# Row maxima across four context quarters: PE transposes replaced by GpSimd copies between partitions, and absorbed query products tied to alternate row halves

## The chip, the cores and the metric

The program runs on one core of a Trainium2 chip. The metric is the device time of one execution in microseconds (us). A core has TensorE (PE, matrix products; PEld is its weight load), VectorE (DVE), ScalarE (ACT), GpSimd (POOL) and SyncE (SP, which issues most DMAs). SBUF and PSUM have 128 partitions. Each engine works through its own instructions in order and waits on semaphores for the others.

## What is computed

Four cross-attention blocks are applied one after the other to `x` (16 batches, 56 tokens, 256 wide) with one context (16 batches, 1500 keys, 128 wide). L0 is a single-head attention with a gate and a norm. L1 and L3 are 16-head attentions with a mask over the keys and a feed-forward part. L2 is a causal self-attention, a 16-head cross-attention over all 1500 keys, and two expert MLPs. In L1 and L3 the core is

```python
sim = jnp.einsum('bhid,bhjd->bhij', q, k)
sim = jnp.where(media_mask[:, None, None, :], sim, neg_inf)
attn = jax.nn.softmax(sim, axis=-1)
out = jnp.einsum('bhij,bhjd->bhid', attn, v)
```

and the softmax of L2's cross-attention is the same without a mask. The mask lets through only padded keys, which all lie among the last 384; the kernel tests for that at run time and takes its short branch, in which L1 and L3 look at 384 keys alone.

## The kernel before, in words

The 16 batches go through each layer in 4 groups of 4 (`G = 4`, 224 tokens a group). The keys of a batch are cut into four quarters (`NQ = 4`). A block of 32 query rows (tokens times heads, `BW = 32`) is multiplied with the four quarters by four products that write the four bands of 32 partitions of one PSUM tile `sc`: partition 32g + r holds query row r against quarter g (L338 to L343). So the maximum of a query row over all keys is a maximum over four partitions that lie 32 apart.

The unit of work is a *period* (`period`, L408): up to 14 such blocks in L1 and L3 (96 keys a quarter, five blocks to one `sc` tile), 8 or 4 in L2 (375 keys a quarter). Three periods are in flight. In period u the kernel

- makes the scores of u on PE (`scores_block`, L340) and copies them to the SBUF tile `p` on DVE, with the mask added and the maximum of each partition taken into `few` (L351 and L355 in L1 and L3; the one instruction of L345 in L2),
- turns the period before, x: exponentials on ACT with the shift as bias and the sum as a second output (`weights_of`, L382), then 32x32 transposes on DVE (`turn_blocks`, L393),
- sums the period before that, y: weights times values on PE (L796 in L1 and L3, L1134 in L2), followed by a copy on ACT.

The shift (minus the maximum over the four quarters, the same in all four bands) is made by `shift_of` in two steps. Step 0: PE transposes the maxima (L362), DVE reduces over the four quarters (L364) and writes the result three more times (L369). Step 1: PE transposes back (L374), and ACT copies the result from PSUM to SBUF (its copies all carry the helper's line L246). In L1 and L3 (`apart`) both steps of u stand in the middle of period u; in L2 the steps of x stand in the first two quarters of the following period. The PSUM tile `t` of the transposes is one of two that `turn()` hands out to many users.

`absorbed` (L693) makes the queries of L1 and L3 for a pair of batches, 16 times in all. Each call makes two groups of eight products (L703); products of even heads read partitions 0 to 63 and write one `t` tile, those of odd heads read partitions 64 to 127 and write the other. ACT (L246) and DVE (L714) copy the tiles to `qa`.

A scheduler orders the instructions of each engine when the program is built, from dependencies and its own estimates; a manual dependency without a semaphore ("NoSync") only fixes an order on one engine. `turn_blocks` has one such tie: turns go after the last copy of scores, or after L369.

Of the kernel before, what the change touches and what calls it, by code (L numbers as in the profile page):

```python
# [62 lines left out]
def tile_kernel(ctx: ExitStack, tc: tile.TileContext, a, layers=4, groups=NG):  # L63
# [29 lines left out]
    def turn():  # L93
        return psum(ps_t, "t")
# [150 lines left out]
    def scalar_copy(out, in_, scale=1.0):  # L245
        nc.scalar.activation(out, in_, AF.Copy, scale=scale)  # L246
# [84 lines left out]
    def scores_block(u, i):  # L331

        sc = psum(ps_s, "sc")
        w, each = u["w"], u["each"]
        some = range(i, min(i + each, u["n"]))
        for j in some:
            at = (j - i) * w
            for g in range(NQ):  # L338
                q, k = u["qk"](j, g)
                nc.tensor.matmul(  # L340
                    sc[g * BW : (g + 1) * BW, at : at + w], q, k, start=True, stop=True,
                    skip_group_check=True,
                )  # L343
        if each == 1:
            return nc.vector.tensor_tensor_reduce(  # L345
                u["p"][:, i, :w], sc[:, :w], u["mask"], 1.0, LOWEST,
                ALU.add, ALU.max, u["mx"][:, i : i + 1],
            ).ins.name
        m = len(some)
        p = u["p"][:, i : i + m]  # L350
        nc.vector.tensor_tensor(  # L351
            p, sc[:, : m * w].rearrange("p (i k) -> p i k", i=m),
            u["mask"].unsqueeze(1).to_broadcast([128, m, w]), ALU.add,
        )
        return nc.vector.tensor_reduce(u["mx"][:, i : i + m], p, AX.X, ALU.max).ins.name  # L355

    def shift_of(u, i):

        n = u["n"]
        if i == 0:  # L360
            u["t"] = turn()
            nc.tensor.transpose(u["t"][:n, :128], u["mx"], ident)  # L362
            nm = small.tile([128, 128], F32, tag="nm", bufs=1, name="nm")[:n]
            nc.vector.tensor_reduce(  # L364
                nm[:, :BW], u["t"][:n, :128].rearrange("k (g r) -> k r g", g=NQ), AX.X,
                ALU.max, negate=True,
            )
            u["nm"] = nm
            return nc.vector.tensor_copy(  # L369
                nm[:, BW:].rearrange("k (g r) -> k g r", r=BW),  # L370
                nm[:, :BW].unsqueeze(1).to_broadcast([n, NQ - 1, BW]),
            ).ins.name
        else:
            nc.tensor.transpose(  # L374
                u["t"][:, 128 : 128 + n], u["nm"], ident[:n, :n]
            )
            u["shift"] = few(n)
            scalar_copy(u["shift"], u["t"][:, 128 : 128 + n])

    def weights_of(u):  # L380
        for i in range(u["n"]):
# [26 lines left out]
    def period(u):  # L408

        x, y = line["turn"], line["sum"]  # L410
        if u:
            n = u["n"]
            blocks = u["blocks"]
            u["p"] = p_tile("p")[:, : n * blocks * BW].rearrange("p (i k) -> p i k", i=n)
            u["mx"] = few(n)
            if u["w"] < blocks * BW:
                nc.gpsimd.memset(u["p"][:, :, u["w"] :], 0.0)
        if y:
# [12 lines left out]
        if u and u["apart"]:  # L431


            for i in range(0, n, u["each"]):
                copied = scores_block(u, i)
            if x and "shift" not in x:
                shift_of(x, 0)
                shift_of(x, 1)
                weights_of(x)
            at = y["blocks"] // 3 if y else 0  # L440
            sums(0, at)
            if x:
                turn_blocks(x, 0, x["n"] // 3, copied)
            copied = shift_of(u, 0)
            sums(at, 2 * at)
            if x:
                turn_blocks(x, x["n"] // 3, 2 * x["n"] // 3, copied)
            shift_of(u, 1)
            sums(2 * at, 3 * at)
            if x:  # L450
                turn_blocks(x, 2 * x["n"] // 3, x["n"], copied)
        else:

            for i in range(4):
                for j in range(2 * i, min(2 * i + 2, n)) if u else ():
                    scores_block(u, j)
                if y:
                    sums(i * y["blocks"] // 4, (i + 1) * y["blocks"] // 4)
                if x and i < 2 and "shift" not in x:
                    shift_of(x, i)  # L460
                    if i:
                        weights_of(x)
                if x and i > 1:
                    at = -(-x["n"] // 2)
                    turn_blocks(x, (i - 2) * at, (i - 1) * at)
# [227 lines left out]
    def absorbed(name, qT, pr):  # L693
# [3 lines left out]
        qa = big.tile([128, 2, N, H], F32, tag="qa", name="qa")  # L697
        for j0 in range(0, 8, 4):

            halves = [turn() for _ in range(2)]  # L700
            for j in range(4):
                for e in range(2):
                    nc.tensor.matmul(  # L703
                        halves[e][:, j * TP : (j + 1) * TP],
                        wkT[e * 64 : (e + 1) * 64, j0 + j, :],
                        qT[e * 64 : (e + 1) * 64, j0 + j, tok],
                        start=True, stop=True,
                    )
            for e in range(2):
                for b in range(2):  # L710
                    src = halves[e][:, : 4 * TP].rearrange("p (j b n) -> p b n j", b=2, n=N)[:, b]
# [665 lines left out]
```

## Time and profile before

| what | value |
|---|---|
| median of 3 runs | 1779.35 us (1778.93 to 1781.23) |
| the profiled execution: time / span | 1781.89 / 1780.0 us |
| mean granted PE clock | 0.986 |
| L0 until about | 178 us |
| L1 mainly | 178 to 500 us |
| L2 mainly | 500 to 1400 us |
| L3 mainly | 1400 to 1780 us |
| L382, exponentials on ACT (x1344) | 588.4 us busy |
| L340, scores on PE, all shapes | 605.2 us busy |
| L703, absorbed products on PE (x512) | 57.1 us busy |
| POOL, whole program | 100.7 us busy, 222 instructions |

An fp32 product leaves two records, so 512 records of L703 are 256 products. Busy times of PE overlap, and the ends of its records are modelled; the distance between the starts of successive records is the safer measure. Periods can be told by L362, L364 and L374, which stand once in each of the 128 periods (64 in L1 and L3, 64 in L2).

### The profile page before, as it was taken

The page shows a single profiled execution, that of the slowest core. Times are in us where ns is not written, and L with a number is a line of the kernel's source. Part 1 is how long each engine was busy: PE and PEld are TensorE (multiplying, and loading weights), DVE is VectorE, ACT ScalarE, POOL GpSimd, SP SyncE. Part 2 cuts the span into 40 slices and gives each one's busy share as a digit, 9 for nine tenths or more (in the row PEclk, how much of TensorE's full clock was granted, in tenths as well). Part 3 has the DMA queues.
Part 4 walks back from the last instruction along what each step waited for, and adds up shares of the span by engine and source line. Part 5 has one row for each costly group of instructions (what it writes and reads, how often), then busy time and mean ns, then how long its engine had stood idle before and what let it go on. Part 6 is the DMA issues. An engine that isn't in the chain of part 4 may idle for free.

```text
span 1780.0 us, 55805 instructions
## 1 busy us (share of the span) xinstructions
PE 1679.9 (94%) x24092; PEld 1109.0 (62%) x24092; DVE 1120.6 (63%) x2726; ACT 1018.4 (57%) x3577; POOL 100.7 (6%) x222
## 2 busy tenths in 40 slices
PE   4888999999899999999999999999999999999997
PEld 3566777776664556555665556556655767777765
DVE  2444866667755666767558675676577656666672
ACT  1443976757454356534755448456454876766763
POOL 0000000000011000000000000000000000000000
PEclk9999999999999999999999999999999999999998
DMA  7431213020030121000321012201200131212120
GB/s 182 132 101 45 76 30 105 23 88 24 28 132 21 37 96 46 21 20 20 99 68 36 5 34 90 78 29 49 91 21 11 34 137 48 92 47 94 44 68 8
DMA packets 60134, 107.08 MB, mean 60 GB/s; under 512 B 7430, under 2 KB 44822, under 8 KB 59878
## 3 DMA queue, kind: packets, MB, share of 16 engines
q1 hardware_dynamic: 58726, 97.27, 16.9%
q0 software_dynamic: 1152, 6.14, 1.4%
q8 instruction: 191, 3.13, 0.7%
q14 instruction: 65, 0.53, 0.1%
HBM read 102.49 MB, written 0.92 MB: 58 GB/s over the span
## 4 chain that ended last, share of the span: by engine, by line
PE 76%; DVE 12%; ACT 5%; DMA 3%; issue 2%; SPq 1%; POOL 1%; DVEq 0%; ACTq 0%; POOLq 0%
PE sc L340 21%; PE o L796 9%; DVE p L393 4%; PE mm L1167 4%; ACT p L382 4%; PE o L1134 4%; PE mm L859 3%; PE mm L847 3%; PE mm L832 3%; PE mm L683 3%; PE t L703 2%; PE mm L1180 2%; DVE p L345 2%; PE t L744 2%; PE t L752 2%; PE mm L883 2%
## 5 line engine op out<-in xcount | busy, mean ns | idle before, releaser
L382 ACT ACTIVATE p<-p,few 128x96 f32<-128x96 f32 (+1 forms) x1344 | 588.4, 440 | 7.1 <-ACT sums L246 0.3
L340 PE MATMUL sc<-kt,qa 128*32 128x375 f32 x3584 | 403.5, 484 | 12.5 <-DVE few L345 11.4
L393 DVE STREAM_TRANSPOSE p<-p 128x480 f32<-128x480 f32 (+3 forms) x319 | 317.2, 1004 | 58.9 <-ACT p L382 57.6
L345 DVE CUSTOM_DVE_ANT_0 p<-sc,no_mask 128x375 f32<-128x375 f32 x448 | 234.6, 534 | 85.0 <-PE sc L340 78.8
L382 ACT ACTIVATION_READ_ACCUMULATOR p<-p,few 128x1 f32 x1344 | 252.7, 188 | 0.0
L340 PE MATMUL sc<-ktl,qa 128*32 128x96 f32 x7168 | 201.7, 249 | 3.3 <-issue 1.7
L340 PEld LDWEIGHTS sc<-kt,qa 128*32 128x32 f32 x3584 | 117.9, 109 | 119.5 <-issue 67.2
L340 PEld LDWEIGHTS sc<-ktl,qa 128*32 128x32 f32 x7168 | 158.2, 110 | 35.5 <-issue 17.7
L1134 PEld LDWEIGHTS o<-p,vc 128*32 128x32 f32 x6144 | 134.7, 110 | 70.1 <-issue 49.8
L796 PE MATMUL o<-p,kvl 128*128 128x448 f32 x384 | 167.6, 565 | 1.1 <-DVE p L393 1.1
L1134 PE MATMUL o<-p,vc 128*32 128x64 f32 (+1 forms) x6144 | 153.0, 215 | 5.4 <-DVE p L393 4.0
L246 ACT ACTIVATE few<-t 128x14 f32<-128x14 f32 (+2 forms) x128 | 22.4, 175 | 233.3 <-PE t L374 233.2
L351 DVE TENSOR_TENSOR p<-sc,mkl 128x480 f32<-128x480 f32 (+1 forms) x192 | 113.8, 607 | 28.5 <-PE sc L340 28.2
L355 DVE TENSOR_REDUCE few<-p 128x5 f32<-128x480 f32 (+1 forms) x192 | 114.3, 612 | 2.8
L796 PEld LDWEIGHTS o<-p,kvl 128*128 128x128 f32 x384 | 67.1, 191 | 55.5 <-issue 45.1
L246 ACT ACTIVATE qa<-t 128x224 f32<-128x224 f32 (+1 forms) x96 | 38.7, 419 | 105.8 <-PE t L703 66.2
L1167 PE MATMUL mm<-xT,w 128*128 128x224 f32 (+1 forms) x384 | 80.9, 360 | 1.4 <-DMA w<-in_L_l_gate 1.0
L1167 PEld LDWEIGHTS mm<-xT,w 128*128 128x128 f32 (+1 forms) x384 | 65.6, 178 | 15.8 <-issue 6.0
L246 ACT ACTIVATE ot<-o 128x448 f32<-128x448 f32 x64 | 33.8, 528 | 54.0 <-PE o L796 54.0
L703 PE MATMUL t<-qT,wl 64*128 64x112 f32 x512 | 57.1, 287 | 2.7 <-DVE qa L714 2.0
L832 PE MATMUL mm<-w,oT 128*112 128x256 f32 x256 | 57.6, 380 | 0.4 <-DVE oT L758 0.4
L703 PEld LDWEIGHTS t<-qT,wl 64*128 64x128 f32 x512 | 49.2, 190 | 13.4 <-DVE qa L714 3.9
(262 smaller groups left out, 2287.6 us busy)
## 6 DMA issues: line engine op xcount, KB each, us to landing
w<-in_L_W SPq DMA_DIRECT2D x16, 1024.0 KB
kt<-in_ctxT SPq DMA_DIRECT2D x16, 768.0 KB
w<-in_L_Wq SPq DMA_DIRECT2D x8, 1024.0 KB
w<-in_L_Wo SPq DMA_DIRECT2D x8, 1024.0 KB
ktl<-in_ctxT SPq DMA_DIRECT2D x32, 192.0 KB
kvl<-in_ctx_last SPq DMA_DIRECT2D x32, 192.0 KB
w<-in_L_v_qkv SPq DMA_DIRECT2D x4, 768.0 KB
w<-in_L_l_qkv SPq DMA_DIRECT2D x4, 768.0 KB
```

The lines of the kernel that those rows point to most:

```text
L246: nc.scalar.activation(out, in_, AF.Copy, scale=scale)
L340: nc.tensor.matmul(sc[g * BW : (g + 1) * BW, at : at + w], q, k, start=True, stop=True, skip_group_check=True,)
L345: return nc.vector.tensor_tensor_reduce(u["p"][:, i, :w], sc[:, :w], u["mask"], 1.0, LOWEST, ALU.add, ALU.max, u["mx"][:, i : i + 1],).ins ...
L351: nc.vector.tensor_tensor(p, sc[:, : m * w].rearrange("p (i k) -> p i k", i=m), u["mask"].unsqueeze(1).to_broadcast([128, m, w]), ALU.add,)
L355: return nc.vector.tensor_reduce(u["mx"][:, i : i + m], p, AX.X, ALU.max).ins.name
L382: nc.scalar.activation(u["p"][:, i, : u["w"]], u["p"][:, i, : u["w"]], AF.Exp, bias=u["shift"][:, i : i + 1], accum_out=u["den"][:, i : i ...
L393: turned = nc.vector.transpose(blocks, blocks)
L703: nc.tensor.matmul(halves[e][:, j * TP : (j + 1) * TP], wkT[e * 64 : (e + 1) * 64, j0 + j, :], qT[e * 64 : (e + 1) * 64, j0 + j, tok], sta ...
L796: nc.tensor.matmul(o[:, : ub * BW], kv[:, j, :], p, start=start, stop=stop)
L832: nc.tensor.matmul(p[:TP, i * D : (i + 1) * D], oT[:, j, i * TP : (i + 1) * TP], wo[:, j, :], start=(j == 0), stop=(j == 7),)
L1134: nc.tensor.matmul(o[cols, : pieces * BW], made["v"][:, j, cols], p.rearrange("p (i g) r -> p g i r", g=4)[:, g], start=start, stop=stop, ...
L1167: nc.tensor.matmul(p[:w, k * T : (k + 1) * T], wt[:, c, cols], xe[n][:, c, :], start=(c == 0), stop=(c == 1),)
```

## The change

`shift_of` no longer uses PE. The tile `mx` gets four slots for each block; the partition maxima go to slot 0. GpSimd copies bands 1 to 3 of slot 0 to slots 1 to 3 of band 0, DVE takes minus the maximum over the slots in band 0, and GpSimd copies that result to the other three bands. The copies on GpSimd are each of 32 partitions by n elements (n = 14, 8 or 4). Both steps stand where step 0 stood. The tie of `turn_blocks` in L1 and L3 now always names the last copy of scores. In `absorbed` each product is tied behind the one before it, so that the two halves of the rows take turns.

```diff
-    def shift_of(u, i):
-        n = u["n"]
-        if i == 0:
-            u["t"] = turn()
-            nc.tensor.transpose(u["t"][:n, :128], u["mx"], ident)
-            nm = small.tile([128, 128], F32, tag="nm", bufs=1, name="nm")[:n]
-            nc.vector.tensor_reduce(
-                nm[:, :BW], u["t"][:n, :128].rearrange("k (g r) -> k r g", g=NQ), AX.X,
-                ALU.max, negate=True,
-            )
-            u["nm"] = nm
-            return nc.vector.tensor_copy(
-                nm[:, BW:].rearrange("k (g r) -> k g r", r=BW),
-                nm[:, :BW].unsqueeze(1).to_broadcast([n, NQ - 1, BW]),
-            ).ins.name
-        else:
-            nc.tensor.transpose(
-                u["t"][:, 128 : 128 + n], u["nm"], ident[:n, :n]
-            )
-            u["shift"] = few(n)
-            scalar_copy(u["shift"], u["t"][:, 128 : 128 + n])
+    def shift_of(u):
+        n, mx = u["n"], u["mx"]
+        shift = u["shift"] = few(n)
+        for g in range(1, NQ):
+            nc.gpsimd.tensor_copy(mx[:BW, g], mx[g * BW : (g + 1) * BW, 0])
+        nc.vector.tensor_reduce(
+            shift[:BW], mx[:BW].rearrange("p g i -> p i g"), AX.X, ALU.max, negate=True
+        )
+        for g in range(1, NQ):
+            nc.gpsimd.tensor_copy(shift[g * BW : (g + 1) * BW], shift[:BW])
...
-            u["mx"] = few(n)
+            u["mx"] = small.tile(
+                [128, NQ, n], F32, tag="mx", bufs=2, name="mx", padded_shape=[128, NQ, US]
+            )
...
-            copied = shift_of(u, 0)
+            shift_of(u)
             sums(at, 2 * at)
...
-            shift_of(u, 1)
             sums(2 * at, 3 * at)
...
-                if x and i < 2 and "shift" not in x:
-                    shift_of(x, i)
-                    if i:
-                        weights_of(x)
+                if x and "shift" not in x:
+                    shift_of(x)
+                    weights_of(x)
...
-            halves = [turn() for _ in range(2)]
+            halves, product_before = [turn() for _ in range(2)], None
             for j in range(4):
                 for e in range(2):
-                    nc.tensor.matmul(
+                    product = nc.tensor.matmul(
                         halves[e][:, j * TP : (j + 1) * TP],
...
+                    if product_before:
+                        tc.add_manual_dep(
+                            product.ins, product_before.ins.name,
+                            mybir.DependencyInfo(
+                                mybir.DependencyClass.NoSync, mybir.DependencyReason.DATA
+                            ),
+                            reason="halves of the rows go in turn",
+                        )
+                    product_before = product
```

More of the change, by code (lines that the diff above doesn't have):

```diff
@@ L346, in scores_block @@
                 u["p"][:, i, :w], sc[:, :w], u["mask"], 1.0, LOWEST,
-                ALU.add, ALU.max, u["mx"][:, i : i + 1],
+                ALU.add, ALU.max, u["mx"][:, 0, i : i + 1],
             ).ins.name
@@ L354, in scores_block @@
         )
-        return nc.vector.tensor_reduce(u["mx"][:, i : i + m], p, AX.X, ALU.max).ins.name
-    def shift_of(u, i):
-        n = u["n"]
-        if i == 0:
-            u["t"] = turn()
-            nc.tensor.transpose(u["t"][:n, :128], u["mx"], ident)
-            nm = small.tile([128, 128], F32, tag="nm", bufs=1, name="nm")[:n]
-            nc.vector.tensor_reduce(
-                nm[:, :BW], u["t"][:n, :128].rearrange("k (g r) -> k r g", g=NQ), AX.X,
-                ALU.max, negate=True,
-            )
-            u["nm"] = nm
-            return nc.vector.tensor_copy(
-                nm[:, BW:].rearrange("k (g r) -> k g r", r=BW),
-                nm[:, :BW].unsqueeze(1).to_broadcast([n, NQ - 1, BW]),
-            ).ins.name
-        else:
-            nc.tensor.transpose(
-                u["t"][:, 128 : 128 + n], u["nm"], ident[:n, :n]
-            )
-            u["shift"] = few(n)
-            scalar_copy(u["shift"], u["t"][:, 128 : 128 + n])
+        return nc.vector.tensor_reduce(u["mx"][:, 0, i : i + m], p, AX.X, ALU.max).ins.name
+    def shift_of(u):
[8 more added lines that the diff above has]
+            nc.gpsimd.tensor_copy(shift[g * BW : (g + 1) * BW], shift[:BW])
     def weights_of(u):
@@ L436, in period @@
             if x and "shift" not in x:
-                shift_of(x, 0)
-                shift_of(x, 1)
+                shift_of(x)
                 weights_of(x)
@@ L458, in period @@
                     sums(i * y["blocks"] // 4, (i + 1) * y["blocks"] // 4)
-                if x and i < 2 and "shift" not in x:
-                    shift_of(x, i)
-                    if i:
-                        weights_of(x)
+                if x and "shift" not in x:
+                    shift_of(x)
+                    weights_of(x)
                 if x and i > 1:
```

## The prediction, before the changed kernel was run

> **What bounds the kernel now.** I read the page's first part for the busiest engine, then the timeline in two typical stretches, then the waits.
>
> ```profile
> PE 1679.9 (94%) x24092; PEld 1109.0 (62%) x24092; DVE 1120.6 (63%) x2726; ACT 1018.4 (57%) x3577; POOL 100.7 (6%) x222
> ```
>
> PE is busy 94% of the span and GpSimd 6%. The average hides two kinds of stretch. In L2, and wherever post and pre of a group lie beside a period, PE is alone at its limit (from 800 to 1400 us it is busy 579 of 600 us, DVE 413, ACT 335). PE around one period of L2:
>
> ```profile
> 917.80 0.27 PE L362 MATMUL t<-ident,few 128*8 128x128 f32 x1
> 918.01 1.47 PE L340 MATMUL sc<-kt,qa 128*32 128x375 f32 x16
> 919.29 0.37 PE L1134 MATMUL o<-p,vc 128*32 128x32 f32 x24
> 919.59 0.22 PE L374 MATMUL t<-ident,nm 8*128 8x8 f32 x1
> 919.75 1.47 PE L340 MATMUL sc<-kt,qa 128*32 128x375 f32 x16
> 921.03 0.37 PE L1134 MATMUL o<-p,vc 128*32 128x32 f32 x24
> 921.22 1.49 PE L340 MATMUL sc<-kt,qa 128*32 128x375 f32 x16
> ```
>
> The same round of two score blocks and three sums lasts 1.47 us from start to start without a transpose (919.75 to 921.22), 1.74 with L374 in it (918.01 to 919.75), and 1.81 with L362 (from the round's start at 916.20 to 918.01).
>
> The other kind is the bare period of L1 and L3. Successive L364 stand 5.54 us apart there; of 128 periods I count 29 like it (5.50 to 5.69). From 235.5 to 252.1 us PE is busy 16.5 of 16.6 us, DVE 16.2, ACT 16.1. DVE, then ACT, across one such seam:
>
> ```profile
> 245.90 0.57 DVE L393 STREAM_TRANSPOSE p<-p 128x384 f32<-128x384 f32 x1
> 246.55 0.28 DVE L364 TENSOR_REDUCE nm<-t 14x32 f32<-14x128 f32 x1
> 246.86 0.24 DVE L369 COPY nm<-nm 14x96 f32<-14x96 f32 x1
> 247.03 1.22 DVE L393 STREAM_TRANSPOSE p<-p 128x480 f32<-128x480 f32 x2
> 248.18 0.60 DVE L351 TENSOR_TENSOR p<-sc,mkl 128x480 f32<-128x480 f32 x1
> ```
>
> ```profile
> 247.24 0.52 ACT L246 ACTIVATE ot<-o 128x448 f32<-128x448 f32 x1
> 247.67 0.16 ACT L246 ACTIVATE few<-t 128x14 f32<-128x14 f32 x1
> 247.86 0.38 ACT L382 ACTIVATE p<-p,few 128x96 f32<-128x96 f32 x1
> ```
>
> DVE has no gap to speak of: its loop sets 5.54. ACT's own loop is 14 exponentials 0.36 apart, 0.43 for `ot` and 0.19 for the shift: 5.65, so ACT falls behind a little in each such period.
>
> ```profile
> ACT few L246 <- PE t L374: 233.2, 86, 8.4
> ```
>
> This longest wait of an engine other than POOL is mostly L2's, where ACT has time to spare; I count nothing for it by itself.
>
> **Transposes off PE in L2.** The rounds above give 0.27 + 0.34 = 0.61 us a period, 39 us for 64. It is on the path, since PE is. What is late next is DVE, which frees the three `sc` tiles. In the shortest period (7.0 us, DVE 0.85 busy, 5.95 us) DVE loses L364 and L369 (0.51) and gains the new reduce plus its wait for GpSimd (0.20 + 0.62, below): 6.26, still under PE's new 6.39. So all 39 us count.
>
> **Transposes off PE in L1 and L3.** L362 and L374 keep PE 0.20 and 0.16 us from start to next start, 0.36; with the interrupted run of scores (112 records take 2.45 us in one piece, 2.98 with L374 and its wait between) it is up to 0.73. In the 35 long periods, where PE is the bound, I take 0.37: 13 us (26 if all counts).
>
> **The new chain.** The trace has no copy on GpSimd between partitions, so its price is open:
>
> ```profile
> L1066 POOL TENSOR_TENSOR spread<-den,tables 128x224 f32<-128x224 f32 x16 | 9.9, 620 | 171.1 <-ACT p L382 141.2 <-PE mm L922 18.7 <-PE sc L340 11.3
> L147 POOL TENSOR_SCALAR mkl<-m32l 128x96 bf16<-128x96 uint8 x32 | 8.7, 271 | 678.3 <-issue 354.8 <-DVE p L351 260.1 <-DMA m32l<-in_mask_last 55.4
> L417 POOL MEMSET p<- 128x36 f32 x16 | 2.1, 131 | 143.5 <-issue 115.2 <-PE o L1134 28.3
> ```
>
> The last numbers before the second bar are mean ns. A memset of one element takes 98 (the constants of L1365); L147 with one input of 96 elements 271, so 1.8 ns an element, and 14 elements give 98 + 25 = 123. The ends are 0.10 and 0.62 (L1066, two inputs, sixteen times as many elements). I take 0.14, near the memset of 36. Three in a row: 0.42. GpSimd starts 0.14 after DVE has finished (L734 to L738 at 252.9 us), and PE 0.05 after GpSimd (L738 to L744); I use 0.06 for DVE and ACT. The new reduce reads 56 elements a partition: a reduce of 3 takes 147 ns (L575), one of 128 takes 276, so 0.20. Last L355 to shift ready: 0.14 + 0.42 + 0.06 + 0.20 + 0.14 + 0.42 + 0.06 = 1.44 us. Before, from the end of L355 (245.98) to the end of the second transpose (247.39) plus ACT's 0.16 it was 1.57. The chain is no longer. 768 copies add 108 us to POOL's 101: not a bound.
>
> **The bare periods.** The order built for the changed kernel puts the reduce behind one turn (L393, 0.57). The copies are ready 0.62 after L355, so DVE waits 0.05 to 0.13 and reduces 0.20, where the old pair held it from 246.47 to 247.03 (0.56): its loop goes to about 5.3. ACT loses the copy and its loop goes to 5.46. So 0.1 to 0.25 a period; 0.15 by 29 is 4 us.
>
> **What is queued behind the new waits.** On DVE, L345, L351 and the turns stand behind the reduce. On POOL, copies stand in order with L147, L738, L1036, L1066 and the memsets L417. In most periods these are ready first. But at the start of each L2 group the built order has a memset whose `p` buffer is freed only by the sums of the running period, ahead of or between that period's copies, and once a group four L1036 (2.2 us) between the two threes. Some 3 such places a group for 4 groups, 0.5 us each on the path after what self-attention hides: -6 us. SP's order is unchanged.
>
> [...]
>
> ```profile
> L1036 POOL TENSOR_TENSOR qs<-l,tables x64: 576/586/1568, 512.7 to 1224.5; 128x224 f32<-128x224 f32 x64
> ```
>
> The 1568 ns (for 586) fell beside L970, a DVE instruction with two SBUF inputs. [...] But the work beside the copies has one SBUF input or reads PSUM (L345, L351, L355, L393); only self-attention and post have others, in long periods. I charge nothing.
>
> **Absorbed products.** Two groups of eight:
>
> ```profile
> 270.88 1.15 PE L703 MATMUL t<-qT,wl 64*128 64x112 f32 x16
> 316.95 1.14 PE L703 MATMUL t<-qT,wl 64*128 64x112 f32 x8
> 318.30 1.81 PE L703 MATMUL t<-qT,wl 64*128 64x112 f32 x16
> ```
>
> Sixteen records (eight products) in turn take as long as eight records of one half. Followed through all 32 groups, one in turn holds PE 1.08 us to the next start, one by halves 1.94; the mean is 1.72. All in turn: 32 x 0.64 = 20 us at most. Against it, a group now needs both `t` tiles free before its second product, while today the copies of one half run under the products of the other: in the call at 271 us, already in turn, the second group starts 1.1 us after the first has ended, though scores fill most of that. I take half, 10 us.
>
> **Sum.** 39 + 13 + 4 + 10 - 6 = 60 us off the profiled 1781.89, which is 2.5 above the median; off the median 1779.35 it is **1719 us**.
>
> **Rivals.**
> *More than that.* The shift of L2 no longer waits for PE's second quarter, so exponentials start about 1 us earlier and turns stop waiting for them (57.6 us of DVE waits, 32 us of PE idle between 500 and 1400). A third of that idle, the full 20 us of L703, 26 us of long periods, no queue loss: about 1687. Against it: the same DVE now waits for GpSimd.
> *The freed time comes back as waits.* DVE's wait for three copies meets `sc` tiles that PE needs at once; half of the L2 and L1/L3 gains go: 1748.
> *Slower: the price of a copy.* At 0.62 us (L1066's) the reduce comes 2.06 us after the last maximum. A bare period's DVE loop is 5.54 - 0.56 + 0.20 + 1.49 = 6.67, 1.13 x 29 = +33; in L2 DVE gets 7.7 for 7.0 us in the short periods and is about even in the others, +20; the 23 us of long periods and L703 still come off, the 6 of the queue stay: +36, 1815. The sums cross zero at about 0.5 us a copy. For it: copies across partitions are shown nowhere. Against it: they are tiny, and every small POOL row is under 0.3.
> *It doesn't do what it says:* 6 of 32 groups are fully in turn already and some partly; in the built order all 32 are. This can only shrink the 10 us.
>
> **How the numbers follow.** Forecast (1700 to 1735) 0.52; more 0.11; waits come back (1735 to 1775) 0.20; within 0.2%, about what a measurement of this kernel can tell from no change, 0.03; slower 0.14, two thirds of it above 1790. Faster is 0.83. The range from 1687 to 1788 leaves out some 0.03 below and 0.10 above.
>
> **What would show it.** Right: copies at 0.1 to 0.2 us, shift to L382 within 1.5 us of the last maximum, bare periods of 5.3 to 5.45, L2's short period near 6.4, all L703 groups near 1.1, PE still the busiest. Wrong: copies above 0.4; reduces waiting on POOL for more than 0.7; PE idle before L340 for DVE growing by tens of us; POOL held by memsets with ACT waiting behind it.

## The result and the profile after

The changed kernel takes 1772.44 us (median of 6 runs, 1768.84 to 1774.54), the kernel before 1779.14 on the same chip: ratio 0.9963, 95% interval 0.9948 to 0.9978. It is faster, by 7 us where 60 were forecast. The ratios leave out runs of more than 1.5% above the fastest of their version: 7 of the 22 of "copies alone" below, and none of any other. The profiled execution took 1768.84 us (span 1767.1), 13.05 us less than the profiled one of before; it is the fastest of its six, and the one of before lies above its six (1776.88 to 1781.23), so the traces show some 6 us more of a gain than the medians. Line numbers below are the changed kernel's: copies L362 and L367, the reduce between them L363, exponentials L371, turns L382, absorbed products L691, and at the end of a pair of batches the product and reciprocal of the sums (L730, L731), `over` on GpSimd (L735) and its product (L741). In the versions of the experiments they are shifted by a few lines.

The shares of the engines in the chain that ended last, before:

```profile
PE 76%; DVE 12%; ACT 5%; DMA 3%; issue 2%; SPq 1%; POOL 1%; DVEq 0%; ACTq 0%; POOLq 0%
```

Busy times and the same shares, after:

```profile
PE 1602.7 (91%) x23836; PEld 1100.2 (62%) x23836; DVE 1089.8 (62%) x2598; ACT 1023.4 (58%) x3470; POOL 247.2 (14%) x990
...
PE 56%; DVE 23%; ACT 9%; DMA 4%; POOL 4%; issue 3%; SPq 0%; POOLq 0%; ACTq 0%; DVEq 0%
```

PE is relieved as meant, 77 us less busy. But its share of the chain fell from 76% to 56%, VectorE's doubled from 12%. And the mean granted clock fell. Before and after:

```profile
core 0: 1780.0 us, clock 0.986
...
core 0: 1767.1 us, clock 0.973
```

The page's row of the clock in 40 slices hides it: in slices of 44 us a few half-clocked microseconds nearly always round to 9.

The new chain in a bare period, to be set beside the seam at 245.90 us of before:

```profile
336.13 0.55 DVE L355 TENSOR_REDUCE mx<-p 128x4 f32<-128x384 f32 x1
...
336.60 0.57 DVE L382 STREAM_TRANSPOSE p<-p 128x384 f32<-128x384 f32 x1
...
336.74 0.68 POOL L362 COPY mx<-mx 32x14 f32<-32x14 f32 x3 [4.01 <-DVE mx L355]
...
337.45 0.23 DVE L363 TENSOR_REDUCE few<-mx 32x14 f32<-32x56 f32 x1 [0.29 <-POOL mx L362]
337.62 1.21 DVE L382 STREAM_TRANSPOSE p<-p 128x480 f32<-128x480 f32 x2
...
337.75 0.67 POOL L367 COPY few<-few 32x14 f32<-32x14 f32 x3 [0.33 <-DVE few L363]
337.79 0.52 ACT L246 ACTIVATE ot<-o 128x448 f32<-128x448 f32 x1
338.45 0.38 ACT L371 ACTIVATE p<-p,few 128x96 f32<-128x96 f32 x1
```

From the end of L355 (336.68) to the first exponential (338.45) it takes 1.77 us: 0.68 and 0.67 for the copies, 0.23 for the reduce, and 0.19 for four hand-offs of 0.03 to 0.07. (The bracket at L367, 0.33, is GpSimd's idle time between its two threes; the reduce is in it.) VectorE now stands idle 0.29 for the copies; such periods last 5.66 to 5.75 us instead of 5.54. Up to the first exponential the way is no longer than it was: at its seam the kernel before took 1.88 us (245.98 to 247.86), because ScalarE made `ot` first. The copies themselves, mean ns before the second bar:

```profile
L367 POOL COPY few<-few 32x14 f32<-32x14 f32 (+2 forms) x384 | 75.1, 195 | 98.6 <-DVE few L363 85.4 <-ACT p L371 0.5
L362 POOL COPY mx<-mx 32x14 f32<-32x14 f32 (+2 forms) x384 | 70.7, 184 | 559.5 <-DVE mx L355 412.2 <-DVE mx L345 133.3 <-DVE cT L929 0.9
```

Then the end of a pair. In the kernel before, the reciprocal (L734 there) ran between the two VectorE steps of `shift_of`, and PE had scores until the product of `over` (L744) could start:

```profile
341.81 0.28 DVE L364 TENSOR_REDUCE nm<-t 14x32 f32<-14x128 f32 x1
...
342.03 0.50 DVE L734 RECIPROCAL den<-t 32x56 f32<-32x56 f32 x1
...
342.45 0.18 DVE L369 COPY nm<-nm 14x96 f32<-14x96 f32 x1
...
342.68 1.90 POOL L738 TENSOR_TENSOR over<-den,tables 32x448 f32<-32x448 f32 x2 [2.03 <-DVE nm L369]
...
343.70 1.94 PE L744 MATMUL t<-over,tables 32*128 32x448 f32 x4
```

After:

```profile
343.21 0.24 DVE L363 TENSOR_REDUCE few<-mx 32x14 f32<-32x56 f32 x1 [0.35 <-POOL mx L362]
343.37 1.22 DVE L382 STREAM_TRANSPOSE p<-p 128x480 f32<-128x480 f32 x2
...
344.52 0.46 DVE L731 RECIPROCAL den<-t 32x56 f32<-32x56 f32 x1
...
345.13 1.90 POOL L735 TENSOR_TENSOR over<-den,tables 32x448 f32<-32x448 f32 x2 [0.96 <-ACT p L371]
...
346.15 2.60 PE L741 MATMUL t<-over,tables 32*128 32x448 f32 x4 [2.63 <-POOL over L735]
```

The reciprocal now stands behind the reduce and both turns, and PE waits 2.63 us. The next lines give stretches of 3.40 us: time, length, then the busy us (with records) of PE, PEld, DVE, ACT and POOL, then the granted clock and two figures on DMA. Before, the stretch with the product of `over`:

```profile
343.10:346.50 3.40, 3.31 (x24) 1.50 (x25) 1.49 (x4) 3.12 (x15) 1.47 (x2) 1.00 0.13 48
```

After, five stretches around the wait:

```profile
340.50:343.90 3.40, 3.02 (x65) 1.87 (x63) 2.98 (x7) 3.40 (x19) 1.18 (x6) 1.00 0.04 8
343.90:347.30 3.40, 1.15 (x3) 0.51 (x4) 3.04 (x7) 2.82 (x16) 2.11 (x4) 1.00 0.27 62
347.30:350.70 3.40, 3.40 (x24) 2.11 (x25) 0.14 (x1) 2.71 (x13) 0.00 (x0) 0.50 0.00 0
350.70:354.10 3.40, 3.40 (x20) 2.94 (x17) 1.91 (x4) 0.77 (x5) 0.00 (x0) 0.50 0.00 0
354.10:357.50 3.40, 3.40 (x20) 3.40 (x19) 0.00 (x0) 1.09 (x2) 0.00 (x0) 0.99 0.00 0
```

After the stretch in which PE was busy 1.15 of 3.40 us, the clock is 0.50 for 6.8 us, in which PE has work all the time. By my estimate, half of these 6.8 us, the wait of 2.63 us costs up to 3.4 us more, later, in instructions that waited for nothing.

**The balance.** In the traces of before and after the recorded clock is always 1.0 or 0.5, in 22 and 40 stretches. Each lasts a multiple of 3.41 us (at 0.5: six of 3.41 and four of 6.83 us before, eleven and eight after), but for the one at the end of the record (4.86 and 5.25 us, at 0.5); I added the stretches at 0.5 ("half clock") and PE's idle time between its first and its last instruction. The stages are cut at the first reduce of the shift of L1, L2 and L3 and at L3's last; idle time goes to the stage in which it begins. The three figures are duration, PE idle, half clock, in us:

| stage | before | after | copies twice | no copies | copies kept, close uncoupled |
|---|---|---|---|---|---|
| L1 | 382.5, 11.7, 13.7 | 379.5, 28.0, 30.7 | 405.0, 46.8, 51.2 | 366.2, 19.1, 20.5 | 363.8, 19.6, 6.8 |
| L2 | 829.5, 28.3, 10.2 | 808.6, 58.1, 13.7 | 859.7, 84.1, 58.0 | 777.3, 35.7, 0 | 800.6, 49.4, 0 |
| L3 | 347.0, 6.7, 3.4 | 359.0, 22.0, 37.5 | 379.6, 42.3, 41.0 | 349.0, 15.6, 23.9 | 338.3, 11.4, 10.2 |
| whole span | 1780.0, 89.8, 52.6 | 1767.1, 154.1, 97.4 | 1865.3, 216.3, 172.8 | 1714.3, 116.0, 63.8 | 1720.5, 123.3, 36.2 |

From before to after PE idles 64 us more, and the half clock lasts 45 us more, which is 22 us of lost work if PE sets the pace. The span fell 13. So about 64 + 22 + 13 = 99 us of PE's work really went. This is a residue, not a measurement: the same sum closes within 2 us from after to "copies twice" (62 + 38 = 100 for 98.2) and to "no copies" (38 + 17 = 55 for 52.8), but overshoots by 15 us for the last column; why is not shown.

The wait for `over` alone: 12 waits of over 1.3 us, 26.6 us in all, each followed within 5 us by 3.4 or 6.8 us of half clock, 61 us in all. With half of that, up to 57 us hang on this one kind of seam.

### The profile page after: what moved, and what is told of

Its sections match the earlier page's. It is cut to its first block, busy times and chain, and to the rows that moved or that the text cites. A ratio compares the mean times of both kernels' runs of the same rounds, so it can differ in the third digit from the quotient of the medians.

```text
span 1767.1 us, 55993 instructions
## 1 busy us (share of the span) xinstructions
PE 1602.7 (91%) x23836; PEld 1100.2 (62%) x23836; DVE 1089.8 (62%) x2598; ACT 1023.4 (58%) x3470; POOL 247.2 (14%) x990
## 4 chain that ended last, share of the span: by engine, by line
PE 56%; DVE 23%; ACT 9%; DMA 4%; POOL 4%; issue 3%; SPq 0%; POOLq 0%; ACTq 0%; DVEq 0%
PE sc L340 12%; ACT p L371 7%; DVE p L382 6%; PE mm L1164 4%; DVE mx L355 4%; DVE p L351 4%; PE mm L856 3%; PE o L793 3%; PE mm L671 3%; PE mm L829 3%; PE t L749 3%; DVE p L345 2%; PE mm L844 2%; PE mm L1177 2%; PE t L741 2%
## 5 line engine op out<-in xcount | busy, mean ns | idle before, releaser
L371 ACT ACTIVATE p<-p,few 128x96 f32<-128x96 f32 (+1 forms) x1344 | 588.6, 441 | 142.4 <-POOL few L367 141.0
L340 PE MATMUL sc<-kt,qa 128*32 128x375 f32 x3584 | 391.0, 485 | 32.2 <-DVE mx L345 32.2
L382 DVE STREAM_TRANSPOSE p<-p 128x480 f32<-128x480 f32 (+3 forms) x319 | 317.4, 1004 | 69.5 <-ACT p L371 69.0
L345 DVE CUSTOM_DVE_ANT_0 p<-sc,no_mask 128x375 f32<-128x375 f32 x448 | 232.2, 536 | 71.4 <-PE sc L340 65.2
L371 ACT ACTIVATION_READ_ACCUMULATOR p<-p,few 128x1 f32 x1344 | 253.6, 189 | 0.0
L340 PEld LDWEIGHTS sc<-kt,qa 128*32 128x32 f32 x3584 | 133.6, 109 | 122.9 <-DVE mx L345 55.6
L340 PE MATMUL sc<-ktl,qa 128*32 128x96 f32 x7168 | 184.6, 249 | 4.5 <-ACT p L371 2.3
L1131 PEld LDWEIGHTS o<-p,vc 128*32 128x32 f32 x6144 | 146.4, 111 | 63.3 <-issue 37.0
L340 PEld LDWEIGHTS sc<-ktl,qa 128*32 128x32 f32 x7168 | 153.4, 110 | 48.7 <-issue 20.6
L362 POOL COPY mx<-mx 32x14 f32<-32x14 f32 (+2 forms) x384 | 70.7, 184 | 559.5 <-DVE mx L355 412.2
L351 DVE TENSOR_TENSOR p<-sc,mkl 128x480 f32<-128x480 f32 (+1 forms) x192 | 115.1, 607 | 42.5 <-PE sc L340 39.3
L355 DVE TENSOR_REDUCE mx<-p 128x5 f32<-128x480 f32 (+1 forms) x192 | 116.8, 614 | 4.4
L246 ACT ACTIVATE sums<-o 128x64 f32<-128x64 f32 x64 | 13.3, 209 | 141.9 <-PE o L1131 141.7
L367 POOL COPY few<-few 32x14 f32<-32x14 f32 (+2 forms) x384 | 75.1, 195 | 98.6 <-DVE few L363 85.4
L1053 PE MATMUL t<-l2w,kt 128*32 128x128 f32 x1536 | 58.8, 274 | 13.9 <-ACT vc L246 13.9
```

The lines of the kernel that those rows point to most:

```text
L340: nc.tensor.matmul(sc[g * BW : (g + 1) * BW, at : at + w], q, k, start=True, stop=True, skip_group_check=True,)
L345: return nc.vector.tensor_tensor_reduce(u["p"][:, i, :w], sc[:, :w], u["mask"], 1.0, LOWEST, ALU.add, ALU.max, u["mx"][:, 0, i : i + 1],). ...
L351: nc.vector.tensor_tensor(p, sc[:, : m * w].rearrange("p (i k) -> p i k", i=m), u["mask"].unsqueeze(1).to_broadcast([128, m, w]), ALU.add,)
L355: return nc.vector.tensor_reduce(u["mx"][:, 0, i : i + m], p, AX.X, ALU.max).ins.name
L362: nc.gpsimd.tensor_copy(mx[:BW, g], mx[g * BW : (g + 1) * BW, 0])
L367: nc.gpsimd.tensor_copy(shift[g * BW : (g + 1) * BW], shift[:BW])
```

## The experiments

Medians are of all runs of a version, ratios against the kernel before on the same chip, with 95% intervals. The medians of the kernel before on these chips lie between 1778.14 and 1779.14 us, so medians of different chips can be compared to about 1 us. Each version is described by its edit; "the balance" is the table above.

### The two parts alone

**Tie alone** (before, with the tie of the absorbed products).

> The kernel before, with the tie of the absorbed queries' products and nothing else. The groups of 16 such products should take 1.35 us in the mean instead of 1.72, as they do after the whole change: 32 x 0.37 = 12 us less of TensorE's time, nothing else moved. If the groups stand on the path: 1779 - 12 = 1767 us (range 1765 to 1771), which would mean that the copies, taken alone, brought nothing or a loss of some 5 us. If the groups are covered by waits of their own (the two PSUM turns that they need): 1777 to 1780, and the whole gain of 7 us comes from the copies.

1775.81 us, ratio 0.9994 [0.9982, 1.0007]: no difference clear of noise; the median lies between the two ranges, nearer the second. The groups do take 1.37 us instead of 1.72, 11 us of PE in all; the time didn't follow.

**Copies alone** (after, without the tie).

> The change without the tie: maxima by GpSimd copies, absorbed products in the order the scheduler gives. The twin of the run with the tie alone: if the two parts add, its time is 1779 - 7 + what the tie gave. With a tie worth 12 us: 1784 us (slower than before); with a tie worth nothing: 1772 us. The forecast on record, with 52 us from the transposes and the periods, would want 1725 us here. TensorE's idle time by stage should stay at 10 + 14 us more in the first and last stage and 32 us more in the third, as after the whole change, since the tie has no part in it.

1791.06 us, ratio 1.0040 [1.0016, 1.0064]: slower than before, so the parts don't add; with the copies in place the tie is worth 15 to 19 us (by the runs that the ratio counts, or by all). The 22 runs of this one program run from 1768.9 to 1801.2 us, and the mean clock of a run goes with them (0.976 down to 0.958, correlation -0.98, 17 us for 0.01, which is 1% of the span). The median clock is 0.9645, against 0.970 after and 0.989 before. This is where I saw that the clock is a term of the sum. A correlation doesn't show which way the cause runs; "close uncoupled" below changes the waits on purpose.

### The length of the chain

**No copies** (each band takes its own negated maximum; both loops of copies are left out).

> The changed kernel without any GpSimd copy: each band of 32 partitions takes its own negated maximum, so the maximum over the four quarters is left out (the exponentials of the quarters are shifted by different amounts). It keeps the order of work as the scheduler gives it without copies. It bounds what the copies' price and hand-offs (1.77 us from the last reduction to the first exponential in a bare period) can cost. Theory 'latency': the time falls by 40 us or more, to 1710 to 1730 us, with periods at 5.3 us. Theory 'clock and order': GpSimd is free for `over` at once, so a part of the waits at the ends of pairs goes, but VectorE's reciprocal still stands behind the turns; 1745 to 1765 us with the clock still below 0.98.

1716.47 us, ratio 0.9646 [0.9625, 0.9668], clock 0.981. "Latency" holds: 56 us, spread over all stages, bare periods at 5.21 us. The clock recovered with it, since the half clock fell by 34 us.

**Copies twice.**

```diff
-            nc.gpsimd.tensor_copy(mx[:BW, g], mx[g * BW : (g + 1) * BW, 0])
+            for _ in range(2):
+                nc.gpsimd.tensor_copy(mx[:BW, g], mx[g * BW : (g + 1) * BW, 0])
...
-            nc.gpsimd.tensor_copy(shift[g * BW : (g + 1) * BW], shift[:BW])
+            for _ in range(2):
+                nc.gpsimd.tensor_copy(shift[g * BW : (g + 1) * BW], shift[:BW])
```

> The changed kernel with each GpSimd copy issued twice: 6 x 0.24 = 1.43 us more on the way from the last score copy to the first exponential, and no other engine's work changed. Leaving all copies out brought 53 us by the two spans (31 in the third stage, 13 and 10 in the second and fourth). Theory 'latency' (what is lost against that is the length of this chain): the price is about even in the chain's length, 53 us for some 2.0 us, so 1.43 us more cost about 38 us, 1800 to 1820 us. Theory 'order and clock' (the copies only rearranged the schedule): the order stays nearly the same and the time stays within 10 us, 1765 to 1782 us.

1867.22 us, ratio 1.0510 [1.0488, 1.0533]: 95 us slower, more than twice what an even price gave. GpSimd is still only 21% busy. By the balance 62 us of the 98 in the spans are PE idle and 38 half clock. The chain's length is on the path, and lost clock comes on top of it.

### The ends of pairs

**Reciprocal early** (product and reciprocal of the sums issued before the turns of that period).

> The changed kernel, with the product and the reciprocal of the sums at the end of a pair of units issued before the turns of that period, and so ahead of the maximum over quarters on VectorE. Theory 'order' (the saved TensorE time came back as waits because the new chain moved other instructions): the wait of TensorE for GpSimd's `over` at the end of each pair in the first and last stages (12 waits of 2.2 us in the mean, 26.6 us) falls below 6 us and the time falls by 15 to 25 us, to 1748 to 1757 us. Theory 'latency' (the copies' chain is longer and the exponentials are late): the wait moves to the next thing behind the exponentials, and the time stays at 1770 to 1774 us.

1780.49 us, ratio 1.0020 [1.0001, 1.0038]: slower than after, and both expectations missed. The timeline at a pair's end (`over` is L741 here):

```profile
246.87 1.89 POOL L741 TENSOR_TENSOR over<-den,tables 32x448 f32<-32x448 f32 x2
...
248.82 0.66 POOL L362 COPY mx<-mx 32x14 f32<-32x14 f32 x3
...
249.51 0.23 DVE L363 TENSOR_REDUCE few<-mx 32x14 f32<-32x56 f32 x1 [1.34 <-POOL mx L362]
```

`over` is now ahead of the copies in GpSimd's queue, and VectorE waits 1.34 us for them, with a turn behind the reduce. PE still waits 1.46 us for `over` here (13.5 us in the whole trace, where "order" wanted under 6), and the half clock rose to 118 us.

**`over` on VectorE** (`nc.vector` for `nc.gpsimd` in L735, order as after).

> The changed kernel, with the two products that make `over` at the end of a pair on VectorE instead of GpSimd; nothing else is edited, but the schedule now puts 28 to 37 score products of the next unit between the product of the sums and the product of `over`. Theory 'clock' (of the 40 us that the change really freed, some 30 went back because the waits of 1.5 to 2.7 us at the ends of pairs bring the half clock: 97 us of it after against 53 before): these waits fall below 1 us, the half clock falls by 40 to 60 us, the mean granted clock rises from 0.970 to 0.980 or more, and the time falls by more than the waits themselves, to 1735 to 1752 us. Theory 'waits alone' (idle time is lost, the clock only drifts from run to run): the 26.6 us of waits fall by at most 20, VectorE has 14 us more to do, and the time is 1755 to 1772 us with the clock at 0.970.

1768.39 us, ratio 0.9940 [0.9919, 0.9962], clock 0.9735. "Waits alone" gave the right size, but not for its reason: PE's idle time stayed at 154.0 us. The wait for `over` halved to 12.8 us, and 7.3 came up at PE's product of `xT` (L671), behind the same VectorE queue.

**A gap in the kernel before** (two ties: reciprocal behind the turns, next scores behind the product of `over`).

> The kernel before, with two ties only: the reciprocal of the sums goes behind the turns of its period on VectorE, and the scores of the next period behind the first product of `over` on TensorE. No work is added or taken away; it puts the wait at the end of each pair, which the changed kernel has, into the kernel before. Theory 'clock': some 12 to 14 waits of about 2 us (25 us of idle) bring 40 to 60 us more of half clock; the mean granted clock falls from 0.989 to 0.97, and the time rises by 35 to 60 us, to 1815 to 1840 us. Theory 'waits alone': 15 to 25 us more, 1795 to 1805 us, and the clock stays at 0.985 to 0.99.

1793.20 us, ratio 1.0066 [1.0042, 1.0089], clock 0.9905. Below both. Sums and transposes took the place of the scores, so only three waits of over 1.3 us came up in L1 and L3; idle time rose 13 us, half clock fell 10. Idle time came at about its own length here, though the fall of the half clock should have given some 5 us back. The run didn't test the clock, as the waits it was to bring mostly didn't come.

**Close later** (from after: what follows `over` at the end of a pair goes behind the next period's scores).

```diff
             for i in range(0, n, u["each"]):
                 copied = scores_block(u, i)
+            later()
...
```

Here `later()` issues the products of `over`, all that follows them, and what was issued before this period's scores.

> The changed kernel, with the products of `over` and all that follows them at the end of a pair issued behind the scores of the next period (and what ran before that period's scores behind it). No work is added or taken away; the 12 waits of TensorE for `over` are filled with scores and absorbed products. Theory 'clock': TensorE's idle time in the second and fourth stage falls from 28 + 22 to some 12 + 7 us, the half clock there from 31 + 38 to some 17 + 10 us, and the time falls by 31 + 20 = 51 us, to 1721 us (1712 to 1735), with the mean clock at 0.98 or more. Theory 'waits alone': 31 us, 1741 us, with the clock at 0.970. Theory 'the length of the copies' chain paces these stages, and TensorE's wait is only where it shows': the wait appears at the next product behind the chain, and the time stays at 1760 to 1772 us.

1765.67 us, ratio 0.9933 [0.9911, 0.9955], clock 0.969. "The chain paces" was right: the wait went to the next product. It needs the PSUM buffer of the sums, which the reciprocal frees, still behind the turns:

```profile
345.70 1.14 PE L697 MATMUL t<-qT,wl 64*128 64x112 f32 x14 [1.83 <-DVE den L735]
```

Of six such waits of about 1.8 us in L1 and L3, five were followed by 13.7 us of half clock and one by none; the total rose to 121.

**Close later, turns tied in L2.**

> As the run before, with the turns of the third stage also tied behind the last score copy of their quarter, which alone took 8 us off the changed kernel (1764.4 us). If the two add: the run before minus 8 us, by 'clock' 1713 us, by 'waits alone' 1733 us, by 'the chain paces' 1752 to 1764 us. The candidate for the fastest kernel that holds the reference's computation.

1756.41 us, ratio 0.9886 [0.9867, 0.9905]: the two edits add about as "the chain paces" had it.

**Close uncoupled** (from the last: product and reciprocal of the sums and `over`, now on VectorE, issued ahead of the turns).

```diff
             sums(0, at)
+            if y and "early" in y:
+                y.pop("early")()
             if x:
                 turn_blocks(x, 0, x["n"] // 3, copied)
...
-                nc.gpsimd.tensor_tensor(
+                nc.vector.tensor_tensor(
...
```

> The run with the close issued later and the turns tied (1756.4 us), with the product and the reciprocal of the sums, and the two products of `over` on VectorE, issued ahead of the turns of that period. In that run the wait had moved to the absorbed product that needs the PSUM buffer of the sums, which VectorE's reciprocal frees (13.9 us, then 13.7 us of half clock each time). Here the reciprocal stands ahead of the turns and nothing of the close is due before the next scores: all waits of over 1.3 us at the ends of pairs should go, in all 25 us of idle with 40 us of half clock. Theory 'clock': 1756 - 20 (idle) - 20 (half of the half clock), 1716 us (1708 to 1728), mean clock at 0.985. Theory 'waits alone': 1736 us. Theory 'the chain paces': the bare periods stay at 5.7 us and the close's VectorE work lengthens it, 1750 to 1760 us, with the idle time again at another product.

**1723.52 us**, ratio 0.9699 [0.9679, 0.9720], clock 0.990: within "clock", outside the other two, and the fastest version that leaves nothing out. All 768 copies are in it. Of 72 us of half clock in L1 and L3 of the run before (between the cuts of the stages), 17 are left. The split was not the expected one, and says more than the total: in the whole trace PE's idle time fell by only 8 us (131 to 123), where 20 were expected, and the half clock by 58 (94.5 to 36.2). PE's busy time for the same 23836 records fell from 1613.4 to 1586.9 us, 27 us, and half of 58 is 29. So of the 34 us between the two spans about a quarter is idle time, and the rest came with the clock. Its span and clock:

```profile
core 0: 1720.5 us, clock 0.990
```

**The same with `over` on GpSimd.**

> As the run before, with the two products of `over` on GpSimd (2 x 0.95 us), where they now stand ahead of that period's six copies in its queue. It isolates GpSimd's queue order, which the forecast put at 6 us in all: at each of 16 ends of pairs the copies start up to 1.9 us later. If that delay is covered by the turns and the scores that follow: within 5 us of the run before. If the chain of copies paces: 1.0 to 1.5 us for each of 16, 16 to 24 us slower than the run before.

1762.03 us, ratio 0.9894 [0.9876, 0.9913]: 38 us slower than with VectorE, where the larger of the two expectations had 16 to 24. At one end of a pair:

```profile
340.49 1.90 POOL L741 TENSOR_TENSOR over<-den,tables 32x448 f32<-32x448 f32 x2
...
342.45 0.64 POOL L362 COPY mx<-mx 32x14 f32<-32x14 f32 x3
...
345.65 0.47 PE L701 MATMUL t<-qT,wl 64*128 64x112 f32 x2 [3.17 <-DVE qa L721]
```

The last maximum is there at 340.75, the copies start at 342.45; PE waits 3.17 us further down. In the whole trace the wait at L701 is 33.9 us (14.9 in the run before), and the half clock 87 us (36).

### The third stage

PE's waits for score copies in L2 before (560 to 1360 us): us in all, times, longest. Then its two largest waits there after; the second didn't show before:

```profile
PE sc L340 <- DVE few L345: 11.4, 20, 1.5
...
PE sc L340 <- DVE mx L345: 32.2, 26, 2.4
PE t L1053 <- ACT vc L246: 13.9, 8, 1.7
```

One of the first kind:

```profile
939.11 0.66 POOL L362 COPY mx<-mx 32x8 f32<-32x8 f32 x3 [0.16 <-DVE mx L345]
...
939.80 0.20 DVE L363 TENSOR_REDUCE few<-mx 32x8 f32<-32x32 f32 x1 [0.83 <-POOL mx L362]
...
940.06 0.65 POOL L367 COPY few<-few 32x8 f32<-32x8 f32 x3 [0.29 <-DVE few L363]
...
940.74 0.61 ACT L371 ACTIVATE p<-p,few 128x375 f32<-128x375 f32 x1 [1.76 <-POOL few L367]
...
943.25 1.78 DVE L382 STREAM_TRANSPOSE p<-p 128x1536 f32<-128x1536 f32 x1 [1.81 <-ACT p L371]
...
945.53 1.47 PE L340 MATMUL sc<-kt,qa 128*32 128x375 f32 x16 [2.41 <-DVE mx L345]
```

The exponentials wait for the copies, a turn of four blocks waits 1.81 us for them on VectorE, the score copies L345 stand behind that turn, and PE waits 2.41 for a free `sc`.

**Turns behind the score copies** (`copied` of the quarter is handed to `turn_blocks` in L2 as well).

> The changed kernel, with the turns of the third stage tied behind VectorE's last copy of scores of their quarter. TensorE's waits for these copies (32.2 us after against 11.4 before, up to 2.4 us in one) come from turns that stand ahead of a copy and wait for late exponentials. Theory 'order': these waits fall to some 10 us, the two to three half-clock periods of the third stage that follow a wait of 2.4 us go (10 us of half clock, 5 us), and the time falls by 15 to 25 us, to 1747 to 1757 us. Theory 'latency' (the exponentials are late whatever stands ahead): the turns come later by what they stood ahead, TensorE waits for the turned blocks instead, and the time is 1770 to 1785 us.

1764.40 us, ratio 0.9911 [0.9886, 0.9936]. "Order" had the place right (the wait fell to 12.1 us, L2's half clock from 13.7 to none) and about half of the size: 8 us, outside both ranges, as PE's waits for turned blocks and for ScalarE's copies of sums rose by 10.

**Exponentials in the second quarter.**

> The changed kernel, with the exponentials of the long units (second and third stages) put into the second quarter of the period, where they were before the change, instead of the first; the copies and the maximum stay in the first. Theory 'order': ScalarE's copies of the values no longer stand behind the exponentials (TensorE's 13.9 us for these copies falls to under 3 us), ScalarE's table loads fall from 53 to some 38 (15 x 1.28 = 19 us less of ScalarE), and the time falls by 5 to 15 us, to 1757 to 1767 us. Theory 'latency': the exponentials come later still, the turns wait longer for them, and the time grows by 5 to 30 us, to 1777 to 1800 us.

1772.39 us, ratio 0.9972 [0.9961, 0.9983]: no change, and no theory hit. The loads of ScalarE's function tables at the exponentials stayed at 53, and PE's second wait went from 13.9 to 12.1 us only. So what this wait costs, and what brought it, is not shown.

**Copies in the third stage alone** (before with the tie of the absorbed products, and GpSimd's copies in L2 only).

> The kernel before with the tie, and GpSimd's copies for the units of the third stage alone; the second and fourth stage keep the two transposes on TensorE. If the stages are independent, the spans add: 176.7 + 378.6 (second stage with the tie alone) + 808.6 (third stage after the change) + 344.3 + 42.4 = 1751 us, range 1744 to 1758, with the mean clock back at 0.980 or more, because the waits at the ends of pairs are gone. If instead the third stage's 21 us came from what the copies did in the neighbouring stages, the time is 1765 to 1775 us.

1762.08 us, ratio 0.9903 [0.9884, 0.9922], clock 0.978. L1 and L3 are back at 378.0 and 348.5 us, L2 at 814.5 with 27 us of half clock. Above the first range, below the second, so neither was hit: the stages nearly add.

**The same with the turns tied.**

> GpSimd's copies in the third stage alone (1762 us), with the turns of that stage tied behind the last score copy of their quarter. TensorE's 30.6 us of waiting for copies of scores in that stage should fall to 12 us, as the tie did in the changed kernel; half clock of 27 us in it to under 7 us. Sum: 1762 - 8 to 1762 - 20, 1748 us (1742 to 1755). If the tie only helped by what it moved at the stage's borders: 1758 to 1763 us.

1743.73 us, ratio 0.9809 [0.9790, 0.9829], clock 0.986. Within the first range; L2 takes 796.4 us.

**VectorE's copies, third stage alone; with the turns tied; in all stages** (the first two from before with the tie, the last from after).

> As the run with GpSimd's copies in the third stage alone, but with these six copies on VectorE, beside the reduction that stands between them: no hand-off to another engine (0.3 us each way). Nearest row for one copy: VectorE's copy of 14x96 in the kernel before, 0.18 us; so 6 x 0.18 + 0.21 = 1.3 us of VectorE for a unit instead of some 2.2 us of chain. Theory 'latency': the third stage falls by 0.9/2.2 of 31 us, 13 us, to 796 us, and the time to 1738 us (1732 to 1745). Theory 'VectorE's queue' (64 x 1.1 = 69 us more on VectorE, which stand ahead of the copies of scores that TensorE waits for): no better than GpSimd's copies, 1750 to 1775 us.

> VectorE's copies in the third stage alone (1762 us), with the turns tied behind the score copies. There the copies of maxima (6 x 0.17 us) stand in VectorE's queue too, ahead of copies of scores, and the tie does not move them. If the turns are what TensorE waits behind: 36.8 us of waiting fall to some 15, and the time to 1745 us (1738 to 1752). If the copies of maxima are: 1755 to 1765 us.

> The changed kernel with all copies, in all stages, on VectorE. In the bare periods of the second and fourth stage VectorE is busy 92 to 98% of 5.7 us, so 6 x 0.18 = 1.1 us more should show: some 0.8 us a period after the 0.3 us idle that it fills, 29 x 0.8 = 23 us more, while the third stage gains 13 us and GpSimd is free for `over` again. Sum: 1772 + 23 - 13 = 1782 us. Theory 'latency alone': shorter everywhere, 1735 to 1750 us. Theory 'VectorE bounds the bare periods': 1775 to 1790 us.

1761.57 us, ratio 0.9919 [0.9899, 0.9938]; 1776.76, 0.9994 [0.9980, 1.0008]; 1812.05, 1.0180 [1.0157, 1.0203]. A copy on VectorE takes 0.167 us in the mean in the first of these runs (0.170 and 0.205 in the last, for the copies of the maxima and of the result). The expectation of the first took the brackets of 0.3 us for hand-offs; the seam above has them at 0.03 to 0.07, so little was to be saved, and VectorE's queue was to pay: PE's wait for L345 is 36.8 us in the first and 35.8 in the second, against 30.6 with GpSimd's copies. "VectorE's queue" holds for the first. The second is outside both of its ranges (the turns were to bring 1745 us, the copies of maxima 1755 to 1765), and why the tie makes it slower is not settled. The last is 30 us beyond its sum and above all three of its ranges: its bare periods take 6.45 to 6.49 us in place of 5.66 to 5.75, and the lower clock (0.968) came on top.

## Why the prediction was wrong, point by point

**Transposes off PE in L2, 39 us: the step that failed is "What is late next is DVE ... 6.26, still under PE's new 6.39. So all 39 us count".** It compared amounts of work and not places in a queue. By the balance, L2 saved 52 us of PE work and got 21, as PE idled 30 more: its waits for L345 grew by 21 us, and those for ScalarE at L1053 came up with 14. VectorE was not full; score copies stood in it behind a turn that waited for exponentials that waited for copies. Tying the turns behind the score copies took 9 us back within L2, leaving the copies out 31.

**Transposes off PE in L1 and L3 and the bare periods, 13 + 4 us.** L1 gained 3 and L3 lost 12. More work was freed than forecast (by the balance 48 us of PE in L1 and L3, the absorbed products' 12 among them), but at the ends of pairs the reciprocal, which had slipped between the two halves of `shift_of`, fell behind the turns. The text named what is queued behind the new wait on VectorE ("L345, L351 and the turns") and left the reciprocal out. With that seam uncoupled and every copy kept, L1 takes 363.8 and L3 338.3 us, and the whole 1723.5 us, within the forecast's 1700 to 1735. That is no proof of its sum: these edits were not run on the kernel before, where they might bring something too.

**The clock: no term at all.** PE's pace was taken as given. By the median clocks, 0.989 and 0.970, and the spread of runs (before: 59 runs, 16 us for 0.01), the clock took back some 30 us. It shares them with the waits that it follows.

**The new chain, 1.44 us, and the bare periods.** The 1.44 came out as 1.77 up to the first exponential. A copy takes 0.184 or 0.195 us in the mean where 0.14 was taken, and three take 0.67 where 0.42 was, which is 0.50 in all; the hand-offs were shorter than taken, 0.19 in all at the seam shown for 0.40. One copy is inside its bounds. "The chain is no longer" set the 1.44 against 1.57, which left out that ScalarE had `ot` to do first; with it the old way took 1.88. What went wrong is the term beside it: VectorE's wait for the copies, taken as "0.05 to 0.13". In the bare periods of 5.74 us VectorE works 5.30, waits 0.34 for the copies and stands 0.10 behind its own L351; before, it was 5.39 and 0.15. So these periods grew by 0.12 to 0.21 us instead of falling by 0.15. As for what the length is worth: "copies twice" lost 95 us for 1.53 us a unit by its trace (the expectation had 1.43), 6 us for each 0.1; "no copies" won 56 us for 1.77 us at most, 3 for each 0.1.

**Queue order on GpSimd, 6 us.** The places named were memsets in L2, and one shows at 938.8. The dear neighbour is `over`, which the text had only in a list: ahead of the copies it costs 38 us ("close uncoupled" with `over` on GpSimd against the same on VectorE).

**GpSimd beside VectorE, nothing charged.** Nearly right for this kernel: the slowest of the 384 copies L362 took 0.24 us, and 11 of the 384 copies L367 took 0.27 to 0.72, eight of them beside a VectorE instruction with two SBUF inputs, 4 us in all. "Close uncoupled" puts such VectorE work (`over`) beside 23 of its copies L362, and these took 0.451 us in the median, the others 0.19. What made them slower there is not shown.

**Absorbed products, 10 us.** 12 us of PE went: a group takes 1.35 us in the mean, not the 1.1 that was to be the sign. Alone they brought no time clear of noise, with the copies 15 to 19 us.

**The rivals.** "The freed time comes back as waits" was the right mechanism at 0.20, and 1772 lies at the edge of its 1735 to 1775. Its size (half the gains, 1748) was too small, since the clock and the reciprocal were not in it.

## What to carry to other kernels

Taking work off the busiest engine is worth nothing until the order of the others is read in the built program: look at every instruction that used to slip into a gap of what you remove, and at what now stands ahead of it. A step that goes through an engine that is nearly idle still has a length, and its queue a neighbour; repeat the step and leave it out to learn its price before arguing. Where half clock follows waits, as it did after all 12 at the seam of `over`, count a wait of the matrix engine up to twice (26.6 us of waits stood beside 61 us of half clock there; that half of it is lost is my estimate), and sum the half-clock time of both traces before explaining a difference.

## What the runs showed of the hardware

- In the traces of before and after the recorded clock was 1.0 or 0.5 only, and half clock came in stretches of 3.41 and 6.83 us, but for the last one (4.86 and 5.25 us); in "close later" one lasted 13.7 us. After each of the 12 waits of 1.6 to 2.7 us for `over` in the trace of after, half clock began within 5 us.
- The half clock can outlast the wait that it follows: after a wait of 1.83 us it stayed for four stretches with PE shown busy 3.36 to 3.40 of 3.40 us in each ("close later").
- In L2 after, only 3 of 12 waits of over 1.3 us for score copies were followed by it, and the place of the wait made the difference in what PE did around it: cut at the changes of the clock, the stretches of 3.41 us around those three have PE busy 0.30, 0.37 and 0.28 of the time, while the nine others spread over stretches that all have 0.41 or more. In the traces of before and after together, each of the 13 stretches at full clock with PE busy under 0.40 was followed by half clock; of 182 between 0.40 and 0.90 it was 16, and of 782 above, none. In all 20 traces it was 120 of 120, 166 of 2058 and 5 of 7416. What decides in the middle isn't shown: at the seam of `over` half clock followed stretches with 0.22 to 0.87.
- A GpSimd copy of 32 partitions to 32 others takes 0.18 to 0.21 us in the mean whether it moves 4 or 14 elements a partition, and the next one starts 0.22 to 0.25 us after its start in most cases.
